# New issue orders for the attention steps of a decoder block, and an earlier load of the second pair's context

## The chip, the core and the metric

The kernel runs on one core of a Trainium2 chip, with all 32 sequences of the batch on that core. The metric is the device time of a run in microseconds (us); lower is better. Times are medians of several runs, and beside them stands one profiled execution with a trace of every instruction.

## The reference

A decoder block in float32 over x of shape (32, 128, 256): causal linear self-attention, cross-attention to a context of the same shape, and a feed-forward part with four gated or GELU layers, each behind a layer norm and with a residual sum. Cut to what matters:

```python
q, k = elu(xn @ Wq.T + bq) + 1, elu(xn @ Wk.T + bk) + 1     # 16 heads of 16
v = xn @ Wv.T + bv
out = sum_{t<=s} (q_s . k_t) v_t / (sum_{t<=s} q_s . k_t + 1e-6)
x = x + out @ Wo.T + bo
attn = softmax(q2 @ k2.T * 0.25)      # q2 from layernorm(x), k2 and v2 from the context
x = x + attn @ v2
h = silu(w1(xn) * s1) * (w2(xn) * s2); h = gelu(h1(h)); h = gelu(h2(h)); x = x + w3(h)
```

## The kernel before

**Tiling.** The batch is worked in 16 pairs of sequences (2 x 128 tokens). Self-attention (functions a_...) of pair m and cross-attention (b_...) of pair m-3 run in the same step m; there are 20 steps (SKEW is 3). The feed-forward part follows in 8 blocks of four sequences; its first block begins beside the last attention steps. Self-attention is computed as masked scores: scores (tile sa) times a causal 0/1 matrix (tile at, line 536) and then times the values (tile pf, line 413), with a column of ones that gives the denominator. Cross-attention computes its scores twice: once for the row maxima (tile sm, then DVE at line 603), and once with the maxima subtracted (tile se, whose last four matmuls add the maxima mT, then the exponential on ACT into tile pr, line 639).

**An order written by hand.** Every function is a generator. It issues one engine's part and yields: a_queries issues its matmuls on PE at the first call, its activations on ACT at the second, the sum on DVE at the third, the masking by heads on POOL at the fourth. A list such as both names units in the order in which they are called, as (function, pairs ahead, half), and give walks through it. So the list sets the order of work on PE, ACT, DVE and POOL, each of which takes its instructions strictly in that order. norms has six calls: three statistics on DVE (with the deviations at the third), the power on POOL, and the normed tiles xna and xnb on POOL. Lists: head ahead of the first step; first0, first1 and first2 for steps 0 to 2, where there is no cross-attention to do yet; both for the full steps 3 to 14; close for step 15; begins, alone, last and rest for steps 16 to 19, in which beside issues a block of feed-forward matmuls and settle its activations.

**Buffers that order the work.** The three kinds of scores of either half share one pair of PSUM tiles (ps_s, two banks each). All other matmul results rotate through four banks (ps_m). The masked scores at have one buffer for each tile of the pair:

```python
at = buffer([P, 2, 4, S], F32, tag=f"at{u}", name="at", bufs=1)
```

One buffer each also have the transposed inputs xTa and xTb, e, r, pr and kb2. The context cT has two. b_load fetches a pair's context (256 KB) from the SP queue:

```python
def b_load(m):
    cT = buffer([P, DC, 2 * S], F32, tag="cT", name="cT")
    nc.sync.dma_start(out=cT, in_=ctxT[:, ts(m, 2 * S)].rearrange("(c p) t -> p c t", p=P))
```

**Names used below.** Projections: tile pp (line 368: a_keys, a_queries, b_keys, b_queries) and pv (line 376: a_values, b_values); pt (line 357) are transposes of normed tiles, pz (line 613) the transpose of the maxima, pot (line 652) that of b_out, pw (line 376) the output projection of a_out. fa and fb (line 430) are transposed results, oa and ob their quotients on POOL, oT and oTb transposed back on DVE (line 445). vb are the context's values in SBUF, kb and kb2 its keys; qa and ka are queries and keys of self-attention. Line 831 is a row of 20 transposes that keeps PE busy till the first data are there.

Of the kernel before, what the change touches and what calls it, by code (L numbers as in the profile page):

```python
# [9 lines left out]
F32 = mybir.dt.float32  # L10
# [6 lines left out]
P = 128  # L17
# [27 lines left out]
def decoder_block_kernel(  # L45
# [222 lines left out]
    with tc.manual_schedule(engines=ORDERED):  # L268
# [24 lines left out]
        cT0 = buffer([P, DC, 2 * S], F32, tag="cT", name="cT")  # L293
# [10 lines left out]
        nc.sync.dma_start(out=row, in_=rows.partition_broadcast(P))  # L304
        load_w(nc.sync, 3)
# [376 lines left out]
        def settle():  # L682
# [9 lines left out]
            (b_keys, 0), (a_norm, 0), (b_keys, 0), (a_norm, 0), (b_values, 0), (a_transpose, 0),  # L692
            (a_norm, 1), (a_transpose, 0), (a_norm, 1), (a_queries, 0), (a_queries, 0), (b_values, 0),
            (a_queries, 0), (a_values, 0), (a_keys, 0), (a_transpose, 1), (a_values, 0), (a_queries, 0),
            (a_keys, 0), (a_transpose, 1), (a_keys, 0),
        ]
        first0 = [
            (norms, 0), (norms, 0), (a_scores, 0, 0), (a_bias, 0), (a_scores, 0, 0), (norms, 0),
            (a_keys, 1), (a_scores, 0, 1), (a_scores, 0, 1), (norms, 0), (norms, 0), (a_weighted, 0, 0),
            (a_keys, 1), (norms, 0), (a_keys, 1), (a_queries, 1), (a_weighted, 0, 0),  # L700
            (a_weighted, 0, 1), (a_values, 1), (a_queries, 1), (a_weighted, 0, 1), (a_queries, 1),
            (a_weighted, 0, 0), (a_transpose, 2), (a_weighted, 0, 1), (a_transpose, 2),
            (a_weighted, 0, 0), (a_values, 1), (a_queries, 1), (a_out, 0, 0), (a_weighted, 0, 1),
            (a_out, 0, 0), (a_bias, 2),
        ]
        first1 = [
            (a_bias, 0), (norms, 0), (a_scores, 0, 0), (a_out, -1, 1), (a_scores, 0, 0), (a_keys, 1),
            (a_out, -1, 1), (norms, 0), (a_keys, 1), (norms, 0), (norms, 0), (a_scores, 0, 1),
            (a_scores, 0, 1), (a_weighted, 0, 0), (a_keys, 1), (a_queries, 1), (norms, 0),
            (a_weighted, 0, 0), (a_weighted, 0, 1), (a_values, 1), (a_weighted, 0, 0), (a_queries, 1),  # L710
            (a_weighted, 0, 1), (a_weighted, 0, 1), (norms, 0), (a_transpose, 2), (a_weighted, 0, 0),
            (a_weighted, 0, 1), (a_values, 1), (a_queries, 1), (a_out, 0, 0), (a_queries, 1),
            (a_transpose, 2), (a_bias, 2), (a_out, 0, 0),
        ]
        first2 = [
            (a_out, -1, 1), (a_out, -1, 1), (a_keys, 1), (a_keys, 1), (a_scores, 0, 0), (norms, 0),
            (b_transpose, 1), (b_transpose, 1), (a_scores, 0, 0), (norms, 0), (norms, 0), (norms, 0),
            (a_values, 1), (a_weighted, 0, 0), (a_scores, 0, 1), (a_weighted, 0, 0), (a_weighted, 0, 0),
            (b_queries, 1), (a_scores, 0, 1), (b_load, 2), (a_values, 1), (a_keys, 1), (norms, 0),
            (b_queries, 1), (a_queries, 1), (a_weighted, 0, 1), (norms, 0), (a_weighted, 0, 0),  # L720
            (a_queries, 1), (a_out, 0, 0), (a_weighted, 0, 1), (a_queries, 1), (a_weighted, 0, 1),
            (b_queries, 1), (a_out, 0, 0), (a_queries, 1), (a_weighted, 0, 1),
# [3 lines left out]
            (a_transpose, 1), (b_maxima, 0, 0), (b_transpose, 1), (b_values, 1), (b_maxima, 0, 0),  # L726
# [59 lines left out]
            (b_out, 0, 0), (norms, 0),  # L786
        ]
        rest = [
            (b_weighted, -1, 1), (b_weighted, -1, 1), (norms, 0), (b_weighted, -1, 1), (norms, 0),
            (b_weighted, -1, 1), settle, beside, (b_out, -1, 1), (b_out, -1, 1), (b_out, -1, 1), settle,  # L790
            (norms, 0),
        ]
# [268 lines left out]
```

## Time and profile before

| what | value |
|---|---|
| median of three runs | 1090.45 us (1090.17 to 1090.6) |
| profiled execution | 1090.98 us |
| its span, first to last instruction | 1088.9 us |
| busy in the span | PE 99%, DVE 55%, POOL 37%, ACT 35% |
| full step (both), start to start | 25.92 us |
| first b maxima (step 3 begins) | at 60.32 us |
| close begins | at 370.98 us |
| begins, alone, last begin | at 392.51, 414.15, 434.97 us |
| granted PE clock | 0.998 over the span |

The attention steps take up to about 456 us, the feed-forward part the rest. In the timeline a row is: start in us, duration in us, engine, line, operation, result<-operands, shapes, count, and in brackets the idle time before it and what ended it. Ends of matmuls are modelled, so the distance between two starts on PE tells more than a duration. In the stretches the columns are: stretch, length, busy time of PE, PE's weight loads, DVE, ACT and POOL with the number of instructions, the granted clock, the DMA share and GB/s. Matmuls on strips (32 of 128 rows for scores, 32 columns for pf) run up to four at a time.

### The profile page before, as it was taken

The numbers are of one execution on the slowest core, as the hardware profiler recorded it, in microseconds if no ns is written. First come the engines' busy times: TensorE is split into PE (matmuls) and PEld (weight loads), VectorE is DVE, ScalarE is ACT, GpSimd is POOL, SyncE is SP. The second block draws the span as 40 slices with busy tenths as digits, with TensorE's granted clock in tenths as the row PEclk, the third lists the DMA queues.
The fourth block names the chain that finished last, engine by engine and source line by source line (L and its number), as shares of the span: only waits on it lengthen the run. The fifth ranks groups of instructions, "written<-read, shape, count | busy, mean of one in ns | idle before, by whom it ended". The sixth has DMA issues, their size and how long they took to land.

```text
span 1088.9 us, 19303 instructions
## 1 busy us (share of the span) xinstructions
PE 1077.3 (99%) x7990; PEld 876.9 (81%) x7990; DVE 599.0 (55%) x1210; ACT 377.8 (35%) x594; POOL 404.8 (37%) x648
## 2 busy tenths in 40 slices
PE   8999999999999999999999999999999999999998
PEld 6777777777777777788888888888888888888887
DVE  4888888888888877523433433433433432423422
ACT  3234444444444459832322322312312312312311
POOL 5555455554544436652312312312312312312311
PEclk9999999999999999999999999999999999999999
DMA  8000001001110000051011011011011000000000
GB/s 266 2 30 31 30 31 31 30 30 39 42 31 30 11 11 2 20 193 35 25 39 34 25 39 35 25 39 39 21 39 39 20 30 20 11 10 20 11 1 23
DMA packets 26542, 39.21 MB, mean 36 GB/s; under 512 B 2512, under 2 KB 18640, under 8 KB 26448
## 3 DMA queue, kind: packets, MB, share of 16 engines
q1 hardware_dynamic: 22000, 26.09, 7.1%
q0 software_dynamic: 4032, 11.54, 3.3%
q8 instruction: 65, 1.06, 0.4%
q10 hardware_dynamic: 416, 0.28, 0.1%
q14 instruction: 29, 0.24, 0.1%
HBM read 33.71 MB, written 4.19 MB: 35 GB/s over the span
## 4 chain that ended last, share of the span: by engine, by line
PE 97%; DVE 2%; POOL 1%; issue 0%; ACT 0%; DVEq 0%; POOLq 0%
PE ph L224 53%; PE pp L368 10%; PE py L885 6%; PE pf L413 5%; PE pv L376 5%; PE sa L397 4%; PE sm L397 3%; PE se L397 3%; PE pw L376 2%; PE pt L357 1%; PE pot L652 1%; PE se L628 1%; PE pz L613 1%; PE pt L213 1%; DVE at L536 1%; PE idle L831 0%
## 5 line engine op out<-in xcount | busy, mean ns | idle before, releaser
L189 DVE TENSOR_TENSOR gl<-hg,gh 128x512 fp32r<-128x512 f32 x126 | 87.3, 693 | 335.0 <-POOL gh L188 332.1
L248 ACT ACTIVATE hg<-ph,col 128x512 f32<-128x512 f32 x128 | 88.3, 690 | 361.3 <-PE ph L224 361.2
L188 POOL CAST gh<-hg 128x512 fp32r<-128x512 f32 x128 | 79.8, 623 | 359.0 <-ACT hg L248 358.9
L224 PE MATMUL ph<-sh,H 128*128 128x512 f32 x512 | 199.6, 390 | 0.0
L224 PE MATMUL ph<-sl,H 128*128 128x512 f32 x512 | 199.3, 389 | 0.0
L224 PE MATMUL ph<-gh,H 128*128 128x512 f32 x512 | 199.2, 389 | 0.0
L224 PE MATMUL ph<-gl,H 128*128 128x512 f32 x512 | 199.2, 389 | 0.0
L224 PEld LDWEIGHTS ph<-sh,H 128*128 128x128 f32 x512 | 96.1, 188 | 20.4 <-issue 0.5
L224 PEld LDWEIGHTS ph<-gl,H 128*128 128x128 f32 x512 | 96.1, 188 | 20.0
L224 PEld LDWEIGHTS ph<-sl,H 128*128 128x128 f32 x512 | 96.1, 188 | 20.0
L224 PEld LDWEIGHTS ph<-gh,H 128*128 128x128 f32 x512 | 96.1, 188 | 19.9
L224 PE MATMUL ph<-xh,W 128*128 128x512 f32 x256 | 100.7, 393 | 0.0
L224 PE MATMUL ph<-xl,W 128*128 128x512 f32 x256 | 99.8, 390 | 0.0
L603 DVE TENSOR_REDUCE nm<-sm 128x8 f32<-128x1024 f32 x64 | 75.2, 1217 | 17.9 <-PE sm L397 17.9
L188 POOL CAST sh<-hs 128x512 fp32r<-128x512 f32 x64 | 58.5, 914 | 69.2 <-DVE hs L240 69.2
L536 DVE TENSOR_TENSOR at<-sa,causal 128x1024 f32<-128x1024 f32 x64 | 74.5, 1206 | 15.6 <-PE sa L397 11.9
L639 ACT ACTIVATE pr<-se 128x1024 f32<-128x1024 f32 x64 | 62.0, 1020 | 29.6 <-PE se L628 29.6
L240 DVE SCALAR_TENSOR_TENSOR hs<-ph,col,sil 128x512 f32<-128x512 f32 x64 | 47.9, 749 | 41.6 <-ACT sil L238 21.0
L495 ACT ACTIVATE e<-pp,col 128x256 f32<-128x256 f32 x64 | 26.9, 470 | 124.7 <-PE pp L368 94.2
L238 ACT ACTIVATE sil<-ph,col 128x512 f32<-128x512 f32 x64 | 44.1, 690 | 74.9 <-PE ph L224 74.8
L368 PE MATMUL pp<-xTa,WA 128*128 128x256 f32 x256 | 62.5, 388 | 0.7 <-ACT xTa L360 0.7
L885 PE MATMUL py<-W,gh 128*128 128x256 f32 x256 | 62.6, 285 | 0.0
(132 smaller groups left out, 1812.8 us busy)
## 6 DMA issues: line engine op xcount, KB each, us to landing
x<-in_x_dram SPq DMA_DIRECT2D x16, 256.0 KB, 5.7
cT<-in_ctxT_dram SPq DMA_DIRECT2D x16, 256.0 KB, 2.6
H<-in_h1T_dram POOLq DMA_DIRECT2D x8, 512.0 KB, 3.6
H<-in_h2T_dram POOLq DMA_DIRECT2D x8, 512.0 KB, 6.7
out_dram<-y SPq DMA_DIRECT2D x32, 128.0 KB, 1.7
raw<-in_h1T_dram SPq DMA_DIRECT2D x16, 256.0 KB, 2.6
raw<-in_h2T_dram SPq DMA_DIRECT2D x16, 256.0 KB, 2.6
WA<-in_wattn_dram SPq DMA_DIRECT2D x4, 256.0 KB, 4.7
```

The lines of the kernel that those rows point to most:

```text
L188: (high_engine.copy if high_engine is nc.scalar else high_engine.tensor_copy)(high, t)
L189: lows.append(lambda: low_engine.tensor_tensor(low, t, high.bitcast(F32), ALU.subtract))
L224: nc.tensor.matmul(pp, lhsT=w[:, k, ts(c, P)], rhs=parts[p], start=(k == 0 and p == 0), stop=(k == len(src) - 1 and p == 1),)
L248: nc.scalar.activation(t, pp, AF.Gelu, scale=col[:, c_scale + c : c_scale + c + 1])
L368: nc.tensor.matmul(pp[:, c, :], lhsT=w[:, d, ts(c, P)], rhs=src[:, d, :], start=(d == 0), stop=(d == DC - 1))
L376: nc.tensor.matmul(pp, lhsT=src[:, d, :], rhs=w[:, d, :], start=(d == 0), stop=(d == DC - 1))
L397: nc.tensor.matmul(sc[g // 2][:, g % 2, 2 * c : 2 * c + 2, :], lhsT=loaded[32 * g : 32 * g + 32, c, ts(j, S)], rhs=streamed[32 * g : 32 * ...
L413: nc.tensor.matmul(pf[32 * g : 32 * g + 32, i, :], lhsT=v[:, 8 * (i // 2) + 2 * g + i % 2, :], rhs=weights[g // 2][:, g % 2, i, :], start= ...
L536: nc.vector.tensor_tensor(at.rearrange("p g i s -> p (g i) s"), sc[u].rearrange("p g i s -> p (g i) s"), causal.unsqueeze(1).to_broadcast( ...
L603: nc.vector.tensor_reduce(nm[:, 2 * u : 2 * u + 2, :], sc[u], AX.X, ALU.max, negate=True)
L639: nc.scalar.activation(pr, sc[u], AF.Exp)
L885: nc.tensor.matmul(py[:, :D], lhsT=h[k][p][:, ts(j, S)], rhs=W3[:, k, :], start=(k == 0 and p == 0), stop=(k == HC - 1 and p == 1),)
```

## The change

The lists head, first0 to first2, both, close, begins, alone, last and rest get other orders of the same units. In both the second half's scores (a_scores, 0, 1) now come ahead of the first half's (a_weighted, 0, 0), with (a_queries, 1) between the first b_weighted and these scores; a_out of the step before comes ahead of the first a_scores; b_load stands at the end of the step. The context of the second pair is loaded in the first row of transfers (cT1), and its b_values is issued in head; so b_load fetches three pairs ahead (3 for 2) in first2 and both, and is gone from close. The work is the same otherwise. The diff, without first1, first2, begins, alone and rest:

```diff
@@ -290,7 +290,7 @@
                 out=WA[:, n] if n < 4 else WB[:, n - 4], in_=wattn[n].rearrange("(c p) o -> p c o", p=P)
             )
 
-        cT0 = buffer([P, DC, 2 * S], F32, tag="cT", name="cT")
+        cT0, cT1 = (buffer([P, DC, 2 * S], F32, tag="cT", name="cT") for _ in range(2))
         load_w(nc.scalar, 5)
         load_x(1)
         nc.sync.dma_start(out=cT0, in_=ctxT[:, : 2 * S].rearrange("(c p) t -> p c t", p=P))
@@ -302,6 +302,7 @@
         load_w(nc.sync, 1)
         load_w(nc.sync, 2)
         nc.sync.dma_start(out=row, in_=rows.partition_broadcast(P))
+        nc.sync.dma_start(out=cT1, in_=ctxT[:, 2 * S : 4 * S].rearrange("(c p) t -> p c t", p=P))
         load_w(nc.sync, 3)
         load_x(2)
         load_w(nc.sync, 4)
@@ -689,105 +690,105 @@
 
         prologue = SKEW
         head = [
-            (b_keys, 0), (a_norm, 0), (b_keys, 0), (a_norm, 0), (b_values, 0), (a_transpose, 0),
-            (a_norm, 1), (a_transpose, 0), (a_norm, 1), (a_queries, 0), (a_queries, 0), (b_values, 0),
-            (a_queries, 0), (a_values, 0), (a_keys, 0), (a_transpose, 1), (a_values, 0), (a_queries, 0),
-            (a_keys, 0), (a_transpose, 1), (a_keys, 0),
+            (b_keys, 0), (a_norm, 0), (b_values, 0), (a_norm, 0), (b_values, 0), (a_transpose, 0),
+            (a_transpose, 0), (a_norm, 1), (a_queries, 0), (b_keys, 0), (a_keys, 0), (a_queries, 0),
+            (a_queries, 0), (a_values, 0), (a_norm, 1), (a_queries, 0), (a_values, 0), (a_keys, 0),
+            (b_values, 1), (b_values, 1), (a_transpose, 1), (a_transpose, 1), (a_keys, 0),
         ]
         first0 = [
-            (norms, 0), (norms, 0), (a_scores, 0, 0), (a_bias, 0), (a_scores, 0, 0), (norms, 0),
-            (a_keys, 1), (a_scores, 0, 1), (a_scores, 0, 1), (norms, 0), (norms, 0), (a_weighted, 0, 0),
-            (a_keys, 1), (norms, 0), (a_keys, 1), (a_queries, 1), (a_weighted, 0, 0),
-            (a_weighted, 0, 1), (a_values, 1), (a_queries, 1), (a_weighted, 0, 1), (a_queries, 1),
-            (a_weighted, 0, 0), (a_transpose, 2), (a_weighted, 0, 1), (a_transpose, 2),
-            (a_weighted, 0, 0), (a_values, 1), (a_queries, 1), (a_out, 0, 0), (a_weighted, 0, 1),
-            (a_out, 0, 0), (a_bias, 2),
+            (norms, 0), (norms, 0), (norms, 0), (a_scores, 0, 0), (a_keys, 1), (norms, 0),
+            (a_scores, 0, 0), (norms, 0), (norms, 0), (a_scores, 0, 1), (a_keys, 1), (a_keys, 1),
+            (a_scores, 0, 1), (a_queries, 1), (a_queries, 1), (a_weighted, 0, 0), (a_weighted, 0, 1),
+            (a_weighted, 0, 0), (a_bias, 2), (a_queries, 1), (a_weighted, 0, 1), (a_bias, 0),
+            (a_transpose, 2), (a_values, 1), (a_weighted, 0, 0), (a_weighted, 0, 0), (a_values, 1),
+            (a_weighted, 0, 1), (a_weighted, 0, 1), (a_out, 0, 0), (a_out, 0, 0), (a_queries, 1),
+            (a_transpose, 2),
         ]
...
         both = [
-            (a_transpose, 1), (b_maxima, 0, 0), (b_transpose, 1), (b_values, 1), (b_maxima, 0, 0),
-            (b_out, -1, 1), (a_scores, 0, 0), (a_transpose, 1), (b_transpose, 1), (b_turn_maxima, 0, 0),
-            (a_scores, 0, 0), (b_out, -1, 1), (a_keys, 1), (b_values, 1), (b_turn_maxima, 0, 0),
-            (w_load, 0), (norms, 0), (a_out, -1, 1), (b_scores, 0, 0), (a_keys, 1), (b_queries, 1),
-            (a_out, -1, 1), (b_scores, 0, 0), (b_queries, 1), (b_maxima, 0, 1), (norms, 0),
-            (b_weighted, 0, 0), (b_out, -1, 1), (b_queries, 1), (norms, 0), (b_maxima, 0, 1),
-            (a_keys, 1), (b_load, 2), (a_weighted, 0, 0), (a_scores, 0, 1), (b_turn_maxima, 0, 1),
-            (a_bias, 1), (norms, 0), (norms, 0), (b_weighted, 0, 0), (a_scores, 0, 1),
-            (b_turn_maxima, 0, 1), (a_weighted, 0, 0), (b_weighted, 0, 0), (a_queries, 1),
-            (a_queries, 1), (b_weighted, 0, 0), (b_keys, 1), (b_scores, 0, 1), (a_values, 1),
-            (a_weighted, 0, 0), (a_weighted, 0, 1), (a_queries, 1), (norms, 0), (b_scores, 0, 1),
-            (a_weighted, 0, 0), (a_values, 1), (a_weighted, 0, 1), (b_weighted, 0, 1),
-            (b_weighted, 0, 1), (b_keys, 1), (b_out, 0, 0), (b_out, 0, 0), (a_weighted, 0, 1),
-            (a_weighted, 0, 1), (b_weighted, 0, 1), (a_out, 0, 0), (b_out, 0, 0), (a_out, 0, 0),
-            (a_queries, 1), (b_weighted, 0, 1),
+            (b_maxima, 0, 0), (b_maxima, 0, 0), (a_transpose, 1), (b_values, 1), (a_transpose, 1),
+            (b_transpose, 1), (w_load, 0), (b_transpose, 1), (a_out, -1, 1), (a_scores, 0, 0),
+            (b_values, 1), (a_out, -1, 1), (b_out, -1, 1), (b_turn_maxima, 0, 0), (a_scores, 0, 0),
+            (a_keys, 1), (b_turn_maxima, 0, 0), (b_scores, 0, 0), (b_out, -1, 1), (a_keys, 1),
+            (b_scores, 0, 0), (b_out, -1, 1), (norms, 0), (b_queries, 1), (norms, 0), (norms, 0),
+            (a_keys, 1), (b_maxima, 0, 1), (norms, 0), (b_weighted, 0, 0), (a_queries, 1),
+            (b_maxima, 0, 1), (a_scores, 0, 1), (a_weighted, 0, 0), (b_queries, 1), (b_weighted, 0, 0),
+            (norms, 0), (a_scores, 0, 1), (b_turn_maxima, 0, 1), (b_keys, 1), (b_turn_maxima, 0, 1),
+            (a_queries, 1), (a_queries, 1), (b_scores, 0, 1), (b_scores, 0, 1), (a_weighted, 0, 0),
+            (a_values, 1), (b_weighted, 0, 0), (b_queries, 1), (b_weighted, 0, 0), (a_bias, 1),
+            (a_values, 1), (a_weighted, 0, 0), (norms, 0), (a_weighted, 0, 1), (b_keys, 1),
+            (b_weighted, 0, 1), (b_out, 0, 0), (a_queries, 1), (b_out, 0, 0), (a_weighted, 0, 0),
+            (a_weighted, 0, 1), (a_weighted, 0, 1), (a_out, 0, 0), (b_weighted, 0, 1),
+            (b_weighted, 0, 1), (a_weighted, 0, 1), (a_out, 0, 0), (b_weighted, 0, 1), (b_out, 0, 0),
+            (b_load, 3),
         ]
         close = [
-            (b_maxima, 0, 0), (b_out, -1, 1), (b_transpose, 1), (a_out, -1, 1), (w_load, 0),
-            (b_maxima, 0, 0), (a_scores, 0, 0), (b_transpose, 1), (b_out, -1, 1), (a_out, -1, 1),
-            (b_values, 1), (a_scores, 0, 0), (b_turn_maxima, 0, 0), (b_turn_maxima, 0, 0),
-            (b_values, 1), (b_scores, 0, 0), (b_scores, 0, 0), (norms, 0), (a_weighted, 0, 0),
-            (b_keys, 1), (b_out, -1, 1), (norms, 0), (b_maxima, 0, 1), (a_weighted, 0, 0),
-            (b_queries, 1), (norms, 0), (b_maxima, 0, 1), (b_load, 2), (norms, 0), (a_scores, 0, 1),
-            (a_scores, 0, 1), (b_turn_maxima, 0, 1), (a_weighted, 0, 0), (b_weighted, 0, 0),
-            (b_turn_maxima, 0, 1), (b_weighted, 0, 0), (b_weighted, 0, 0), (a_weighted, 0, 0),
-            (b_scores, 0, 1), (b_queries, 1), (b_keys, 1), (a_weighted, 0, 1), (b_weighted, 0, 0),
-            (a_weighted, 0, 1), (a_out, 0, 0), (norms, 0), (b_queries, 1), (a_out, 0, 0), (b_out, 0, 0),
-            (b_scores, 0, 1), (b_out, 0, 0), (a_weighted, 0, 1), (b_out, 0, 0), (norms, 0),
+            (b_transpose, 1), (b_maxima, 0, 0), (a_out, -1, 1), (b_out, -1, 1), (b_maxima, 0, 0),
+            (a_scores, 0, 0), (a_out, -1, 1), (b_turn_maxima, 0, 0), (b_out, -1, 1), (b_transpose, 1),
+            (a_scores, 0, 0), (b_values, 1), (b_turn_maxima, 0, 0), (b_scores, 0, 0), (b_scores, 0, 0),
+            (w_load, 0), (norms, 0), (a_weighted, 0, 0), (norms, 0), (b_out, -1, 1), (norms, 0),
+            (b_maxima, 0, 1), (a_weighted, 0, 0), (a_weighted, 0, 0), (b_maxima, 0, 1),
+            (b_weighted, 0, 0), (norms, 0), (b_values, 1), (b_queries, 1), (a_scores, 0, 1),
+            (b_turn_maxima, 0, 1), (b_weighted, 0, 0), (a_scores, 0, 1), (b_turn_maxima, 0, 1),
+            (b_queries, 1), (a_weighted, 0, 0), (b_keys, 1), (b_weighted, 0, 0), (norms, 0),
+            (b_keys, 1), (b_weighted, 0, 0), (b_queries, 1), (b_scores, 0, 1), (a_weighted, 0, 1),
+            (b_out, 0, 0), (b_scores, 0, 1), (a_weighted, 0, 1), (a_out, 0, 0), (a_weighted, 0, 1),
+            (norms, 0), (b_out, 0, 0), (a_out, 0, 0), (b_out, 0, 0),
         ]
...
         last = [
-            (b_maxima, 0, 0), (b_maxima, 0, 0), (norms, 0), settle, beside, (b_weighted, -1, 1),
-            (b_weighted, -1, 1), (b_weighted, -1, 1), (b_turn_maxima, 0, 0), (b_turn_maxima, 0, 0),
-            (b_scores, 0, 0), settle, (b_scores, 0, 0), (b_weighted, -1, 1), (norms, 0), beside,
-            (b_weighted, 0, 0), (b_out, -1, 1), settle, (b_maxima, 0, 1), (b_weighted, 0, 0), beside,
-            (b_maxima, 0, 1), (b_turn_maxima, 0, 1), (b_weighted, 0, 0), (b_out, -1, 1),
-            (b_weighted, 0, 0), (b_turn_maxima, 0, 1), (b_out, -1, 1), settle, (b_scores, 0, 1),
-            (norms, 0), (norms, 0), (norms, 0), (b_out, 0, 0), beside, (b_scores, 0, 1), (b_out, 0, 0),
-            (b_out, 0, 0), (norms, 0),
+            (b_maxima, 0, 0), (b_maxima, 0, 0), (b_weighted, -1, 1), (b_turn_maxima, 0, 0),
+            (b_weighted, -1, 1), settle, beside, (norms, 0), (b_weighted, -1, 1), (b_turn_maxima, 0, 0),
+            (norms, 0), (b_weighted, -1, 1), settle, (b_scores, 0, 0), beside, (b_scores, 0, 0),
+            (b_out, -1, 1), (b_weighted, 0, 0), settle, (b_weighted, 0, 0), (b_out, -1, 1),
+            (b_maxima, 0, 1), (b_maxima, 0, 1), beside, (b_out, -1, 1), (b_turn_maxima, 0, 1),
+            (b_weighted, 0, 0), (b_turn_maxima, 0, 1), (b_scores, 0, 1), (b_weighted, 0, 0),
+            (b_out, 0, 0), settle, (b_scores, 0, 1), (b_out, 0, 0), (norms, 0), (norms, 0), beside,
+            (norms, 0), (norms, 0), (b_out, 0, 0),
         ]
...
@@ -820,8 +821,8 @@
             for c in range(FILLS - 1 - HC)
         ]
 
-        Bs[0]["c"] = cT0
-        done = {(b_load, 0)}
+        Bs[0]["c"], Bs[1]["c"] = cT0, cT1
+        done = {(b_load, 0), (b_load, 1)}
         constants()
         for v in (vb[0], va[0], va[1], vb[1]):
             fill(v)
```

## The prediction

> **What bounds the kernel now.** I read the page's chain first: its share by engine is nearly all TensorE.
>
> ```profile
> PE 97%; DVE 2%; POOL 1%; issue 0%; ACT 0%; DVEq 0%; POOLq 0%
> ```
>
> A chain of 97% PE does not say that PE is short of nothing: a matmul that waits between its first and last part counts as busy. The stretches show that the full steps repeat every 25.92 us, with DVE busy 22.68 us in each.
>
> ```profile
> 203.84:229.76 25.92, 25.92 (x306) 20.18 (x302) 22.68 (x49) 11.65 (x21) 13.29 (x23) 1.00 0.10 32
> 229.76:255.68 25.92, 25.92 (x306) 20.19 (x302) 22.68 (x49) 11.64 (x21) 13.28 (x23) 1.00 0.10 32
> ```
>
> So I went to the timeline of one full step, PE's rows and then DVE's, and measured from start to start. The three kinds of scores (sm, sa, se) share one pair of PSUM tiles, so each must be emptied before the next is filled.
>
> ```profile
> 203.84 1.61 PE L397 MATMUL sa<-qa,ka 32*128 32x256 f32 x16
> 205.38 0.33 PE L613 MATMUL pz<-ident,z 128*128 128x128 f32 x1
> ...
> 209.10 1.15 PE L397 MATMUL se<-qb,kb 32*128 32x256 f32 x16
> ...
> 215.88 1.15 PE L397 MATMUL sm<-kb,qb 32*128 32x256 f32 x16
> ...
> 219.49 1.15 PE L397 MATMUL sa<-qa,ka 32*128 32x256 f32 x16
> ...
> 220.67 2.36 DVE L536 TENSOR_TENSOR at<-sa,causal 128x1024 f32<-128x1024 f32 x2 [0.83 <-PE sa L397]
> ...
> 223.42 1.15 PE L397 MATMUL se<-qb,kb 32*128 32x256 f32 x16
> ...
> 226.65 1.29 PE L397 MATMUL sm<-kb,qb 32*128 32x256 f32 x16
> ```
>
> The reader is to see two things. Masking takes 1.18 + 2.36 = 3.54 us from the start of a self-attention score, so se cannot be filled entirely before +3.59 (DVE's end to the next weight load is about 0.05). And only one score of the step is visibly held: the sa at 203.84 needs 1.54 us to the next operation, the sa at 219.49 only 1.07 (next start 220.56). The 0.47 is the wait for the maxima (L603, done at 204.27). Everything else is PE's own cadence. (Columns: start, duration, engine, line.)
>
> Next, two places at the start of the trace:
>
> ```profile
> 18.82 1.15 PE L397 MATMUL sa<-qa,ka 32*128 32x256 f32 x16 [2.04 <-DVE ka L500]
> 19.90 3.58 PE L368 MATMUL pp<-xTa,WA 128*128 128x256 f32 x8
> ...
> 20.00:23.40 3.40, 3.40 (x8) 2.19 (x8) 2.57 (x5) 0.00 (x0) 0.71 (x1) 0.52 0.71 248
> ...
> 38.13 1.08 PE L413 MATMUL pf<-at,va 128*32 128x128 f32 x32
> ...
> 39.25 2.36 DVE L536 TENSOR_TENSOR at<-sa,causal 128x1024 f32<-128x1024 f32 x2 [0.76 <-PE pf L413]
> ...
> 41.66 1.07 PE L413 MATMUL pf<-at,va 128*32 128x128 f32 x28 [0.18 <-DVE at L536]
> ```
>
> First: PE idles 2.04 us before the first scores, and then a projection takes 3.50 us to the next start instead of 1.82, at a granted clock of 0.52. Second, the row on which this forecast rests: the at tiles have one buffer each, and where the second masking of a pair is put before the first pf has read them, the masking waits for that pf to end. From the pf's start to the next PE work that needs the result: 41.66 - 38.13 = 3.53 us.
>
> **The full steps (m = 4 to 14, eleven of them).** No operation is added or removed, so I lay the new PE order out with the cadences of the present step: projection 1.73 (1.82 ahead of a score or behind one; 1.92 ahead of sm or pf), score 1.07 ahead of whole-array work or of pf, sm behind pr 1.23 (its own 0.16 wait included), mT part .53 after the .78 of its scores, pf .90 ahead of pf, 1.01 ahead of a projection (24.53 to 25.54), .99 ahead of pot, pw .96 ahead of a score and .87 otherwise, pot .27, pz .17, pt .44 to .53. From score to score:
>
> - sm0 to sa0: before 3.61. New: sm 1.08, pt .49, b values 1.73, pt .44, pw .96 = 4.70. The maxima are ready at about 3.6 to 3.9, so no wait.
> - sa0 to se0: before 3.93. New: 1.07, pot .27, pz .17, keys 1.82 = 3.33; the pw that stood here has gone ahead of sa0. Below the 3.59 of masking: wait .26, so 3.59.
> - se0 to sm1: 3.23 both times.
> - sm1 to sa1: before 3.11, and then .47 inside sa1. New: 1.23, pf of b 1.01, the a queries 1.92 = 4.16. DVE has the three statistics (3.65) and now ka ahead of the maxima; these end about 3.8 after sm1's start, so the .47 is gone.
> - sa1 to se1: before 5.26 (with that .47). New: 1.07, then the pf of a, 1.01, pz .17, b keys 1.82 = 4.07. But this pf is the one that reads the at tiles, so masking starts only at its end: 1.07 + 1.08 + .03, two times 1.18, .05 = 4.59, as in the rows at 38 to 41 us. Wait .52. mT follows on DVE at 5.2, in time for its matmul at 5.37.
> - se1 to the next sm0: before 6.78. New: .78, .53, a values 1.92, .90, .99, .27, pw .96 = 6.35.
>
> Before 25.92, new 26.62: +0.70 a step, of which +.31 is waits (.26 + .52 - .47) and +.39 cadence (the array goes between row strips, column strips and whole use 16 times instead of 14). Eleven steps: +7.7.
>
> What could add to it: each queue is reordered too. DVE idles some 1.3 us at the new wait; behind it stand mT, the queries' e, fa and the rest. Walked through, fa of the first half ends 0.8 us before pf needs its bank, oT 0.9 before pw, and oTb is late by 0.3 into the next step's maxima, where sa0 has slack of about 0.8. DVE's 22.7 of work plus 1.3 is below 26.6. POOL (13.3 busy) makes qa 4 us ahead of its use. ACT's kb tiles free pot's bank as now (212.85 + 1.29 against pot at 214.21), the order from se1 to pot being the same. So I add nothing for these; the cover is the slack named, and beyond it (0.8 us for oTb and oT) the step loses the excess.
>
> **Loads.** The context load moves from the middle of a step to its end, but fetches one pair further ahead: it has nearly a step where a load lands in 2.6 us. Its wait (for the keys that last read the buffer) holds up only SP, and SP has nothing else to do till the output. At the start one more issue (about 0.5 us of SP) and 256 KB (0.7 us at 383 GB/s) come ahead of WO, the third pair and XQ. x of the third pair then lands near 12 us and is read at 18, WO is read at 32. Cost 0; lower bound 0, upper bound 0.7 if something were that close.
>
> **Head and first steps.** In the head the second pair's values (1.73) go ahead of the first scores. ACT puts vb ahead of xTa (+0.1), and kb, kb2 between xTa and the exponentials: the keys' bank is free at 12.85 instead of 12.7. PE then runs on: queries 11.0, keys 12.9, values 14.6, b values 16.3, transposes 18.1, first scores about 18.6, where ka (17.8) and qa (16.7) are ready. So the 2.04 idle is filled. By the Trainium skill, "TensorE: Matmul & The Clock Gate", section "HAM oscillation — how this bites in real kernels", only PE gaps above about 3.4 us matter to the clock; then filling 2.04 us is worth those 2.04 at most. The row above disagrees: after 2.04 us of idleness the clock was about half for 3.4 us, and the projection took 1.68 longer. I take the row, so 1.7 more.
>
> The new first step gives it back. Its queries stand ahead of the first pf, so (same at tiles) the second masking starts at 26.2 instead of 25.64 and the second pf goes on at 28.6 instead of 28.05; PE has only four matmuls between 26.0 and 28.6. From there to the second pair's keys: 35.2 against 35.24 now. The second and third step come out the same way: the first b maxima at 60.5 against 60.32, with one transpose (.5) owed and the values done. The first full step lacks those values but its sa0 must wait for the maxima (3.58 after sm0), so it gains only 1.1 of the 1.73 against the new steady step: 25.5. Sum to its end, the owed transpose counted: +0.1. Bounds: -3.4 if both fillings came through (1.73 + 1.68), +1.7 if the gap at 26 to 28.6 halves the clock once more (by the skill's rule it would not, by the row it can).
>
> **The last steps.** close now has its scores 1.3 behind the first maxima, 0.4, 1.2 and 0.5 later on; walked likewise it takes 22.2 us against 21.6: +0.6. begins and alone hang on ACT's table loads (three and a half us each around a silu), whose number is unchanged: -0.2. In last, pz now stands ahead of settle and of a block of eight matmuls, and waits about 1.8 us for the maxima on DVE, half of it made up: +0.9. Bounds of the three: -1.5 and +3. The feed-forward part (from 460 us) is untouched.
>
> **Sum.** +0.1 + 7.7 + 0.6 + 0.7 = +9.1 us. The profiled execution took 1090.98 (span 1088.9 and 2.1 around it), so 1100.1; the median of the runs is 0.5 lower, so 1099.5.
>
> **Rivals.** (1) Other side: the score tiles' halves are released one by one and four matmuls start ahead, so the .26 and .52 are hidden; the old .47 is gone all the same and cadence costs less than counted. A step then takes 25.8 or less, eleven give -1 to -3, and the head gives -1.5: about 1087.5. For it: DVE has 3 us of slack a step. Against it: in the rows at 38 to 41 us just this wait held PE despite those four matmuls. It decides where a step falls under 25.8. Chance 0.11. (2) A second bound: DVE's late oTb and oT push maxima and pw, each step loses 0.3 to 0.6 more (eleven times: 3 to 7 us), the clock's 1.7 on top at worst: 1103 to 1107. For it: nearly every DVE slack above is under 1 us. Chance 0.12. (3) The new order is a wash, the waits about .2 in all, steps at 25.9 to 26.1: 1090 to 1092.5. Chance 0.09. That the change doesn't do what it says is no rival here: orders are issued as written.
>
> **Numbers.** The forecast itself, +0.4 to +0.95 a step, has 0.68 and covers 1095 to 1102.5. 0.2% is 2.2 us, about what a measurement of this kernel can tell from no change: faster 0.10, same 0.08, slower 0.82. The range 1091.5 to 1104.5 leaves out most of rival 1 and the upper part of rival 2.
>
> **What would show it.** In the changed trace: the period of full steps at 26.6; at (L536) waiting for pf (L413) about 1.2 us once a step; se held by DVE at twice a step, and the sa behind the second maxima no longer split; no clock dip at 20 us; a wait of PE near 26 to 28.6 us. A period at 25.9 or less, or an at that does not wait for pf, would make the prediction wrong.

## The result and the profile after

The changed kernel takes 1097.51 us (median of 4 runs, 1096.6 to 1098.02), the kernel before in the same session 1090.53 (4 runs, 1090.17 to 1090.81): a ratio of 1.0064, interval 1.0052 to 1.0076. It is 7.0 us slower. The forecast was 1099.5. The profiled execution took 1097.93 us with a span of 1095.8, so 6.9 us more span than before (1088.9).

All lines of the code stand one lower than before: scores L398, pf L414, at L537, maxima L604.

In the chain of the changed kernel, TensorE's share is still nearly everything, so by that view nothing has happened:

```profile
PE 96%; DVE 1%; issue 0%; ACT 0%; POOL 0%; DMA 0%; SPq 0%; POOLq 0%; DVEq 0%
```

The stretches do tell it. Here are two full steps, from one sm to the same sm of the next step (length; busy time and count of PE, PEld, DVE, ACT, POOL; granted clock; DMA share; GB/s):

```profile
192.99:219.45 26.46, 26.46 (x303) 20.02 (x302) 22.48 (x49) 11.53 (x21) 13.32 (x23) 1.00 0.11 32
219.45:245.92 26.47, 26.47 (x303) 20.04 (x303) 22.48 (x49) 11.53 (x21) 13.33 (x23) 1.00 0.10 31
```

A step has nearly the same work (weight loads 20.0 us against 20.2 before, DVE 22.5 against 22.7) and takes 26.465 us instead of 25.92 (the mean of ten steps, 87.13 to 351.79). PE counts as busy in all of it, although it waits: the waits lie within groups of matmuls. The timeline of PE in the first of these steps shows them as cuts (start, duration, engine, line, operation):

```profile
192.99 1.15 PE L398 MATMUL sm<-kb,qb 32*128 32x256 f32 x16
...
197.68 1.15 PE L398 MATMUL sa<-qa,ka 32*128 32x256 f32 x16
...
200.96 1.23 PE L398 MATMUL se<-qb,kb 32*128 32x256 f32 x14
...
202.57 1.99 PE L369 MATMUL pp<-xTb,WB 128*128 128x256 f32 x8
...
204.49 1.16 PE L398 MATMUL sm<-kb,qb 32*128 32x256 f32 x16
...
208.51 1.15 PE L398 MATMUL sa<-qa,ka 32*128 32x256 f32 x16
209.59 1.08 PE L414 MATMUL pf<-at,va 128*32 128x128 f32 x32
210.60 0.33 PE L614 MATMUL pz<-ident,z 128*128 128x128 f32 x1
...
212.59 1.44 PE L398 MATMUL se<-qb,kb 32*128 32x256 f32 x14
214.41 1.99 PE L377 MATMUL pv<-WA,xTa 128*128 128x256 f32 x8
```

Both se are broken after 14 of their matmuls (x14 where an undisturbed one shows x16). The first needs 1.61 us to the next operation, the second 1.82, where an undisturbed one needs 1.31 (16 matmuls on strips in 0.78 us, four at a time, where 8 on the whole array take 1.73; then the four for the maxima): waits of 0.30 and 0.51. The sa behind the second maxima, which was cut before, is whole. The first cut is the one that was forecast: masking ends 3.54 us after its score starts, and se comes after 3.28. DVE's timeline has the reason for the second; the bracket is the idle time before the operation and what ended it:

```profile
210.71 2.35 DVE L537 TENSOR_TENSOR at<-sa,causal 128x1024 f32<-128x1024 f32 x2 [1.13 <-PE pf L414]
```

The masking starts 1.12 us after pf does, at its end, not at the end of the scores. DVE keeps to the listed order meanwhile: the inputs of the queries' sum e were ready at 210.19 (the end of L498 on ACT), with DVE idle, and e ran at 213.58, behind the masking. The list of costliest groups names the new releaser too (busy in all, ns of one; then the idle time ahead and what ended most of it). First the kernel before, where it was the scores, then the changed one:

```profile
L536 DVE TENSOR_TENSOR at<-sa,causal 128x1024 f32<-128x1024 f32 x64 | 74.5, 1206 | 15.6 <-PE sa L397 11.9
L537 DVE TENSOR_TENSOR at<-sa,causal 128x1024 f32<-128x1024 f32 x64 | 75.3, 1218 | 26.1 <-PE pf L414 17.0
```

The trace of the tile se names DVE's masking as what PE's weight loads for se waited for 13 times (3.0 us in all); in experiment 1 below, only once (0.2 us).

At the start, PE's timeline of the changed kernel and three stretches (same columns as above):

```profile
18.03 1.15 PE L398 MATMUL sa<-qa,ka 32*128 32x256 f32 x16
19.11 1.99 PE L369 MATMUL pp<-xTa,WA 128*128 128x256 f32 x8
...
24.61 1.08 PE L414 MATMUL pf<-at,va 128*32 128x128 f32 x32
...
27.00 0.41 PE L414 MATMUL pf<-at,va 128*32 128x128 f32 x4 [1.31 <-DVE at L537]
28.13 1.57 PE L414 MATMUL pf<-at,va 128*32 128x128 f32 x28 [0.72 <-DVE at L537]
```

```profile
20.00:23.40 3.40, 3.40 (x25) 2.28 (x24) 2.23 (x3) 1.57 (x4) 3.16 (x7) 1.00 0.83 287
26.00:30.00 4.00, 2.28 (x34) 1.61 (x35) 3.93 (x7) 0.28 (x1) 0.72 (x1) 0.82 0.00 0
30.00:34.00 4.00, 4.00 (x16) 3.15 (x14) 2.02 (x6) 0.59 (x1) 3.18 (x6) 0.76 0.00 0
```

The 2.04 us of idleness before the first scores are gone, and so is the half clock at 20 us. In their place PE idles 1.31 + 0.72 = 2.03 us in the first step, again for the masking, and the clock falls there. The first sm stands at 61.95 (before 60.32).

From there the starts of sm give the account, after against before:

| start of | after | before | difference |
|---|---|---|---|
| the first sm of step m = 4 | 87.13 | 86.27 | +0.86 |
| the same sm ten steps on | 351.79 | 345.49 | +6.30, so +5.44 in ten steps |
| begins' sm (behind the last full step and close) | 399.85 | 392.51 | +7.34 |
| alone's sm | 421.37 | 414.15 | +7.22 |
| last's sm | 441.16 | 434.97 | +6.19 |
| the sm after it | 451.91 | 445.00 | +6.91 |

The new list has its sm one transpose (0.5) earlier in the slot than the old one, so the first part really owes +1.36, and the eleventh step (+0.55) and close (about 0) make up the rest of the third row. Most of the loss is in the full steps. These are single executions: PE's second projection starts at 7.43 us here and at 7.89 before, where PE's order is still the same.

### The profile page after: what moved, and what is told of

Read it like the earlier page. It is cut to its first block, busy times and chain, and to the rows that moved or that the text cites. A ratio compares the mean times of both kernels' runs of the same rounds, so it can differ in the third digit from the quotient of the medians.

```text
span 1095.8 us, 19355 instructions
## 1 busy us (share of the span) xinstructions
PE 1082.6 (99%) x7990; PEld 875.2 (80%) x7990; DVE 596.4 (54%) x1210; ACT 375.7 (34%) x594; POOL 405.7 (37%) x648
## 4 chain that ended last, share of the span: by engine, by line
PE 96%; DVE 1%; issue 0%; ACT 0%; POOL 0%; DMA 0%; SPq 0%; POOLq 0%; DVEq 0%
PE ph L224 53%; PE pp L369 10%; PE py L886 6%; PE pf L414 5%; PE pv L377 5%; PE se L398 4%; PE sa L398 3%; PE sm L398 3%; PE pw L377 2%; PE pt L358 1%; PE se L629 1%; PE pot L653 1%; PE pt L213 1%; DVE nm L604 1%; PE pz L614 1%
## 5 line engine op out<-in xcount | busy, mean ns | idle before, releaser
L537 DVE TENSOR_TENSOR at<-sa,causal 128x1024 f32<-128x1024 f32 x64 | 75.3, 1218 | 26.1 <-PE pf L414 17.0
L604 DVE TENSOR_REDUCE nm<-sm 128x8 f32<-128x1024 f32 x64 | 74.7, 1207 | 7.9 <-PE sm L398 7.9
L886 PE MATMUL py<-W,gl 128*128 128x256 f32 x256 | 62.0, 283 | 0.0
```

The costliest lines, as they stand in the source:

```text
L537: nc.vector.tensor_tensor(at.rearrange("p g i s -> p (g i) s"), sc[u].rearrange("p g i s -> p (g i) s"), causal.unsqueeze(1).to_broadcast( ...
L604: nc.vector.tensor_reduce(nm[:, 2 * u : 2 * u + 2, :], sc[u], AX.X, ALU.max, negate=True)
L886: nc.tensor.matmul(py[:, :D], lhsT=h[k][p][:, ts(j, S)], rhs=W3[:, k, :], start=(k == 0 and p == 0), stop=(k == HC - 1 and p == 1),)
```

## The experiments

**1. Two buffers for the first at tile.** The disputed wait is removed by what makes it: with a second buffer the masking need not wait until pf has read the first. The first at tile alone gets one, and qa gives up its second buffer to make room. The order of the work is that of the changed kernel.

```
- two = buffer([P, DC, 2, 2 * S], F32, tag=tag, name=tag)
+ two = buffer([P, DC, 2, 2 * S], F32, tag=tag, name=tag, bufs=1 if tag == "qa2" else 2)
...
- at = buffer([P, 2, 4, S], F32, tag=f"at{u}", name="at", bufs=1)
+ at = buffer([P, 2, 4, S], F32, tag=f"at{u}", name="at", bufs=2 - u)
```

> The changed kernel with two buffers for the first of the two at tiles (and one in place of two for qa, to make room). The second masking can then begin while pf still reads the first half's scores. My theory (masking waits for pf, and se waits for masking): the wait of at for pf, 1.13 us a step, and the 0.52 us by which the second se of a step is held are gone; a full step takes 25.95 us in place of 26.47; eleven steps give 5.7 us, and the first step's gap shrinks: 1097.5 falls to about 1091.5. Rival (the loss is the extra switching between row strips, column strips and the whole array, and the waits are covered): period 26.3 to 26.5, time 1096 to 1098. Rival of the second bound (DVE): the wait comes back elsewhere, period 26.2 or more.

Measured: 1089.08 us (21 runs), ratio to before 0.9993 (0.9986 to 0.9999). By the ratios that is 0.7% or 7.7 us below the changed kernel: the whole loss. PE's timeline of one step, and DVE's masking in it:

```profile
229.60 1.15 PE L398 MATMUL sa<-qa,ka 32*128 32x256 f32 x16
230.67 1.08 PE L414 MATMUL pf<-at,va 128*32 128x128 f32 x32
...
233.67 1.15 PE L398 MATMUL se<-qb,kb 32*128 32x256 f32 x16
234.98 1.99 PE L377 MATMUL pv<-WA,xTa 128*128 128x256 f32 x8
```

```profile
230.78 2.36 DVE L537 TENSOR_TENSOR at<-sa,causal 128x1024 f32<-128x1024 f32 x2
```

The masking starts 1.18 us after sa instead of 2.20, with no idle bracket, se is whole, and 1.31 us on comes the next operation. The period is 25.955 (214.07 to 240.02): 0.51 less, just the wait that was seen. The other cut, se behind the first masking, was still there (222.05 to 223.64, 1.59 us), since it does not come from the buffer:

```profile
222.05 1.23 PE L398 MATMUL se<-qb,kb 32*128 32x256 f32 x14
...
223.64 1.99 PE L369 MATMUL pp<-xTb,WB 128*128 128x256 f32 x8
```

Twelve steps (m = 3 to 14) give 6.1. Another 2.3 in the two profiles (8.4 together) are ahead of them (first sm at 59.63 instead of 61.95), where the same wait stood: more than had been expected. The time fell 2.4 us below the expected 1091.5.

**2. The same buffers in the kernel before (control).** If at's second buffer were good in itself, experiment 1 would prove little.

> The kernel before the change with two buffers for the first at tile and one for qa, the same edit as in the first experiment. My theory: in the old order pf reads the first half's scores ahead of the second half's sa, so in the full steps nothing waits for the at buffers: period 25.92 as before; only the first steps, where pf stood behind that sa, gain: 1089.3 to 1090.5. Rival (a second buffer is worth as much in any order): period 25.4 or less, 1085.

Measured: 1089.01 (13 runs), ratio 0.9984 (0.9976 to 0.9992). The period stayed at 25.92. The gain of about 1.7 us is all ahead of the full steps (first sm at 58.52 instead of 60.32). In the profiles 0.28 of it stands already at the first sa (18.54 instead of 18.82). So in the old order the full steps do not wait for this buffer; the new order made the wait.

**3. The wait of the first se.** Here the projection pw goes back between sa0 and se0, where it stood before.

```
- (a_out, -1, 1), (a_scores, 0, 0), (b_values, 1), (a_out, -1, 1), (b_out, -1, 1),
+ (a_scores, 0, 0), (b_values, 1), (b_out, -1, 1),
...
+ (a_keys, 1), (a_out, -1, 1), (b_turn_maxima, 0, 0), (b_scores, 0, 0), (a_out, -1, 1), (b_out, -1, 1),
```

> The changed kernel with the output projection of the step before (a_out, -1, 1) put back between the keys and the first se of the full steps, where it stood before the change. My theory: se then comes 0.9 us later after sa, masking (3.54 us) is done, the 0.30 us by which the first se is held is gone, and the score ahead of it still comes no sooner than the maxima are ready (3.83 against 3.75 us): period 26.17, eleven steps give 3.3 us: 1094.2. Rival (cadence alone): 26.4 to 26.5, 1097. If the maxima are late: sa is held instead, period 26.3 to 26.5.

Measured: 1097.13 (5 runs), ratio 1.0059 (1.0045 to 1.0072): the expected total was missed. PE's timeline of a step:

```profile
226.60 1.15 PE L398 MATMUL se<-qb,kb 32*128 32x256 f32 x16
...
227.91 1.99 PE L369 MATMUL pp<-xTb,WB 128*128 128x256 f32 x8
229.84 1.30 PE L398 MATMUL sm<-kb,qb 32*128 32x256 f32 x16
231.06 1.08 PE L414 MATMUL pf<-pr,vb 128*32 128x128 f32 x32
```

The first se is whole, 1.31 us to the next operation: the 0.30 is gone. But now sm takes 1.22 us to the next start instead of 1.09. The exponentials pr, which empty the score tiles, end at 229.95 here, 0.11 after sm starts; in the changed kernel they end 0.03 ahead of it (204.46 and 204.49), because the held se had delayed sm. Half of the gain goes to this next wait: the period is 26.30 instead of 26.465, where 26.17 was expected. In its profile the eleven steps give 1.8 us (begins' sm at 398.03 instead of 399.85, with the sm of step 4 where it was), and `last` takes 1.6 of it back: from its sm to the next 12.32 us instead of 10.75, at a clock of 0.93 and 0.73 in the two stretches of 5 us there. The list `last` is the same in both kernels (see below).

**4. pf taken away from between the scores.** In place of another buffer, another order: the pf that reads at goes ahead of the queries and sa1. Its transposition on DVE, further down in the list, moves ahead too.

```
- (a_queries, 1), (b_maxima, 0, 1), (a_scores, 0, 1), (a_weighted, 0, 0), (b_queries, 1),
+ (a_weighted, 0, 0), (a_queries, 1), (b_maxima, 0, 1), (a_scores, 0, 1), (b_queries, 1),
```

> The changed kernel with the first pf of self-attention ahead of the queries and of the second half's sa in the full steps (and its transposition on DVE ahead of the queries' e, so that its bank is free in time). Masking no longer waits for pf, but only pz and one projection are left between sa and se, 3.06 us against the 3.59 that masking takes. My theory: the second se is held by 0.53 all the same, a step takes 26.3 to 26.4 us, time 1096. Rival (the wait for pf alone held se): period 25.85, 1090.5.

Measured: 1096.76 (4 runs), ratio 1.0049 (1.0034 to 1.0065), with a period of 26.33, as expected. PE's timeline, then DVE's:

```profile
207.95 1.15 PE L398 MATMUL sa<-qa,ka 32*128 32x256 f32 x16
209.03 0.33 PE L614 MATMUL pz<-ident,z 128*128 128x128 f32 x1
...
211.02 1.44 PE L398 MATMUL se<-qb,kb 32*128 32x256 f32 x14
212.84 1.99 PE L377 MATMUL pv<-WA,xTa 128*128 128x256 f32 x8
```

```profile
209.13 2.35 DVE L537 TENSOR_TENSOR at<-sa,causal 128x1024 f32<-128x1024 f32 x2 [1.03 <-PE sa L398]
```

The masking starts 1.18 us after sa, as in experiment 1, and yet se is cut and takes 1.82 us. With pf gone, PE arrives at se after 3.07 us, and the masking needs 3.59 before the score tiles are free. It is the same 0.5, now for the score tiles. pf was both what delayed the masking and what PE did meanwhile. Of the two remedies tried, the buffer takes the one and leaves the other; no run put other work between sa and se.

**5. The old full steps in the changed kernel.** What do the other parts cost alone? `both` is that of before, with the load at its end.

> The changed kernel with the full steps' order of before (only the load of the context stays at the end of the step, three pairs ahead). My theory: the loss is in the eleven full steps: period 25.92, time 1091.0 to 1091.7; what is left is the head and the first steps. Rival (the loss is in the head, the first and the last steps): 1095 or more.

Measured: 1094.47 (5 runs), ratio 1.0035 (1.0021 to 1.0048): a miss, 3 us above what was expected and nearer to the rival's 1095. The period is 25.92. But begins' sm stood at 394.67, 2.2 us behind the kernel before, all from the first steps (first sm at 62.46); and the first full step took 25.89, although the values of the second pair were done: PE reached sa0 earlier and waited for the maxima. Another 1.6 us came in `last`, where the clock fell to 0.66 and sm to sm took 12.35 us instead of 10.75.

**6. The first steps: gap and clock apart.** Experiments 6a and 6b part the two. 6a lays 18 transposes with unused results into the gap, which leaves the wait of the masking but keeps PE busy. 6b removes the wait: the first pf goes ahead of the two blocks of queries. The rule that 6a's expectation sets against its theory is the one that the prediction quotes.

```
6a: - (a_queries, 1), (a_weighted, 0, 0), (a_weighted, 0, 1),
    + (a_queries, 1), (a_weighted, 0, 0), keep_busy, (a_weighted, 0, 1),
6b: - (a_scores, 0, 1), (a_queries, 1), (a_queries, 1), (a_weighted, 0, 0), (a_weighted, 0, 1),
    + (a_scores, 0, 1), (a_weighted, 0, 0), (a_queries, 1), (a_queries, 1), (a_weighted, 0, 1),
```

> The changed kernel with 18 transposes of the identity between the first pf of the first step and the second, where PE stands idle for 2.3 us (they are extra work, read by nobody, 1.9 us at full clock). My theory (the idle time halves the granted clock from 28 to 32 us[...]): the clock stays at 1.00, the first maxima of cross-attention come at 60.4 us in place of 61.95, and the time falls by 1.2 to 1.7 us: 1096. By the rule[...]: no change, or slower by up to 0.5 us.

> The changed kernel with one unit moved in the first step: the first pf ahead of the second pair's queries instead of behind them. My theory (the second masking waits for that pf, so the queries in between delay everything after): masking of the second half starts at 23.8 instead of 26, the second pf goes on at 26.2 instead of 28.1, PE has no idle gap there, the clock stays at 1.00 from 26.8 to 33.6 us, the first maxima come at 59.5 to 60.3 us, and the time falls by 1.2 to 1.8 us: 1095.7 to 1096.3. Rival (another wait, for qa or oT, takes its place in the second step): 1097 or more.

Measured: 6a 1097.09 (5 runs), ratio 1.0061 (1.0047 to 1.0074); 6b 1095.45 (5 runs), 1.0043 (1.0029 to 1.0057). 6a's total missed the expected 1096; 6b's came out a little below what was expected. The first pf rows of 6b:

```profile
22.60 1.08 PE L414 MATMUL pf<-at,va 128*32 128x128 f32 x32
...
26.12 1.07 PE L414 MATMUL pf<-at,va 128*32 128x128 f32 x28 [0.18 <-DVE at L537]
```

The second pf goes on at 26.12 instead of 28.13. In 6a's profile the first sa stands 0.9 us later than in the changed kernel's, ahead of anything that the edit touches. The stretch from the first sa to the first sm is free of that, and with it the runs with this first step fall into three sets:

| | first sa | first sm | between |
|---|---|---|---|
| gap, clock reduced: changed kernel | 18.03 | 61.95 | 43.92 |
| the same: experiment 8 | 17.94 | 61.87 | 43.93 |
| gap, clock 1.00: experiment 3 | 18.94 | 61.27 | 42.33 |
| the same: experiment 4 | 18.85 | 61.17 | 42.32 |
| gap filled with transposes, clock 1.00: 6a | 18.97 | 61.30 | 42.33 |
| wait removed: 6b | 17.95 | 58.31 | 40.36 |
| wait removed by the buffer: experiment 1 | 18.99 | 59.63 | 40.64 |

(Experiment 5 is left out: in its list one more transpose stands ahead of the first sm.) The wait costs 1.7 to 2.0 us, and the reduced clock 1.6 more where it comes. 6b cuts both from the changed kernel's profile (3.56). The median fell by only 2.1: in 6b's profile, too, the clock fell in `last`, to 0.69 (sm to sm 12.29).

**7. The new head alone, in the kernel before**, with the load that it needs:

> The kernel before the change with only its new head and the early load of the second context: the second pair's values are projected ahead of the first scores, all later orders as before. What the head gains: no 2.04 us of idle PE ahead of the first scores and no halved clock from 20 to 23.4 us; first maxima of cross-attention at 58.6 us in place of 60.3. My theory: the values were hidden in the wait for the maxima of the first full step, so that step stays at 25.9 us and their 1.73 us are not gained a second time: 1088.7 to 1089.3. Rival (the head is worth both, 3.4 us): 1087. Rival (it is worth nothing, the first steps give it back even in the old order): 1090.3 or more.

Measured: 1090.13 (13 runs), ratio 0.9998 (0.999 to 1.0006): no difference that can be measured, where 1088.7 to 1089.3 was expected. PE's timeline at the first full step:

```profile
58.74 1.15 PE L398 MATMUL sm<-kb,qb 32*128 32x256 f32 x16
59.81 0.66 PE L358 MATMUL pt<-ident,xnb 128*128 128x128 f32 x4
62.33 1.18 PE L398 MATMUL sa<-qa,ka 32*128 32x256 f32 x16 [1.86 <-DVE nm L604]
```

The clock at 20 to 23.4 us is 1.00 instead of 0.52, and the first sm comes 1.58 us earlier. The values (1.73) that were projected early bring nothing on top: the first full step still takes 25.95, because sa0 waits 1.86 us for the maxima just where they stood. The profiled execution (1089.19) keeps the 1.58 to its end; in the median it isn't seen. The clocks on record tell part of why: the seven runs with a clock of 0.999 or 1.000 over the span took 1089.2 to 1090.1, the six with 0.998 took 1090.6 to 1091.0. The kernel before does the same without the new head: in all comparisons together, its seven runs with 1.000 took 1089.4 to 1089.7, its forty with 0.998 took 1090.2 to 1091.9. So much of what the new head gives in its profile may be a dip of the clock that the kernel before does not have in every execution. Where the clock fell in the six is open, as only one run has a trace.

**8. The old `last` in the changed kernel.**

> The changed kernel with the order of before in the last step but one (the list last). My theory: PE's wait for z ahead of pz, 1.9 us, goes, half of which was made up later: -0.9, and the clock cannot drop there any more: 1096.0 to 1096.7. Rival (the last steps play no part): 1097.3 or more.

Measured: 1097.62 (5 runs), ratio 1.0058 (1.0045 to 1.0072): no gain, a miss. In `last`, sm to sm takes 10.55 us with the old list, 10.75 with the new, 10.03 in the kernel before. ACT's timeline of this experiment:

```profile
441.43 1.28 ACT L238 ACT_TABLE_LOAD   x1
...
443.43 1.28 ACT L81 ACT_TABLE_LOAD   x1
...
448.35 1.92 ACT L640 ACTIVATE pr<-se 128x1024 f32<-128x1024 f32 x2
```

PE's rows of it (the transpose of the maxima, then the pf that reads pr):

```profile
445.81 0.33 PE L614 MATMUL pz<-ident,z 128*128 128x128 f32 x1 [0.42 <-DVE hs L240]
...
450.32 1.07 PE L414 MATMUL pf<-pr,vb 128*32 128x128 f32 x28 [0.16 <-ACT pr L640]
```

The long wait ahead of pz (1.90 us in the changed kernel) is gone with the old list, and yet only 0.2 us come back. ACT has no gap from 439.20 to 453.69; two silu with two table loads each (1.28 us a load) stand in line ahead of pr, and PE waits for pr. So 0.5 of the 0.7 that `last` loses is not in its list. PE comes out of `alone` 1.0 us sooner, and ACT does not: in the kernel before it starts the first of these loads at 433.88, 1.09 us ahead of sm, and then idles 0.73 for se ahead of pr; here it starts it at 441.43, 0.29 behind sm. What would make ACT's part shorter was not tested.

**9. Better versions.** 9a joins the buffers of experiment 1, pw of experiment 3 and the old `last`. 9b is the kernel before with the same buffers and only the full steps of 9a (its context load after the keys), so against experiment 2 it changes the full steps alone.

> The changed kernel with two buffers for the first at tile (one for qa), the pw of the step before back ahead of the first se, and the old list last. My theory: period 25.78 (25.955 of the first experiment, less the 0.30 of the first se, plus 0.13 that sm then waits for the exponentials), eleven steps give 1.9 us, last another 0.9: 1086.3. Rival (DVE, at 22.7 us a step, or the score tiles set a floor of 25.9): 1088.2 or more.

> The kernel before the change (its head, first steps, closing steps and loads) with two buffers for the first at tile, one for qa, and only the full steps of the best version so far (the changed order with pw back ahead of the first se). My theory: the good of the change lies in its full steps once at has a second buffer, and its head, first and last steps are worth nothing in sum: period 25.79, time 1087.2 to 1087.8, as the best version. Rival (the changed head and ends are worth 1.5 us): 1088.8 or more.

Measured: 9a 1087.57 (6 runs, 1087.14 to 1088.01), ratio 0.997 (0.9957 to 0.9982); 9b 1087.71 (9 runs, 1086.4 to 1088.31), 0.9974 (0.9964 to 0.9984). Both beat both kernels, and neither the other. 9b is within what was expected. A step takes 25.79 us in both. One step of 9a on PE:

```profile
213.61 1.15 PE L398 MATMUL sm<-kb,qb 32*128 32x256 f32 x16
...
221.59 1.15 PE L398 MATMUL se<-qb,kb 32*128 32x256 f32 x16
...
224.82 1.29 PE L398 MATMUL sm<-kb,qb 32*128 32x256 f32 x16
...
233.05 1.15 PE L398 MATMUL se<-qb,kb 32*128 32x256 f32 x16
```

No se is cut any more. So the new order of the full steps, freed of its two waits, is 0.13 us a step better than the old one, and the new head, first and closing lists are worth nothing in sum that these runs could tell (9a against 9b). 9a missed its expectation by 1.3 us, most of it the 0.9 that experiment 8 had been supposed to give and did not.

## Why the prediction was right

Its main step holds: at waits for pf once a step (1.13 us; 1.2 was named), that cuts se by 0.51 (0.52), and the other se by 0.30 (0.26). Experiment 1 shows that it is this wait and decides sign and size: without it, the kernel is not slower. The old cut of 0.47 is gone, as said. That the total came so near (6.9 us in the profiles against 9.1) is in part luck: the first part came out 1.3 us dearer than forecast, the other terms 3.4 cheaper. By its own terms:

- **Full step, +0.70.** Measured +0.545. From score to score (predicted, then measured): 4.70, 4.69; 3.33, 3.28; 3.49, 3.53; 4.16, 4.02; 4.07, 4.08; 6.87, 6.86. One term was mis-sized, sm1 to sa1, which charged sm 0.16 for a wait for pr. With se held for 0.30 just before, pr is ready (0.03 us ahead of sm). Experiment 3 shows the two to be one exchange: free se and sm waits. Eleven steps: +6.0 in place of +7.7.
- **First part, +0.1.** Measured +1.36. The filling of the 2.04 gap worked, clock included, and the new gap in the first step came where it was put (26 to 28.6 predicted, 25.7 to 28.1 seen). The term that failed is its clock, valued at 0 with 1.7 as the upper bound. The upper bound came true: 43.92 - 42.33 = 1.6. With it, and with the 0.5 by which this execution was ahead before the orders differ, the forecast would have been 0.1 + 1.6 - 0.5 = 1.2. The Trainium skill ("TensorE: Matmul & The Clock Gate", "HAM oscillation — how this bites in real kernels") gives as its rule "no PE-idle gaps >~3.4µs"; by it the shorter gaps here would cost only their own length, but two idle stretches of 1.31 and 0.72 us were followed by a lower clock in three profiles, and in two others not (last section). The prediction had rejected that rule for the gap before the first scores, from the trace, and then spared the new gap what its own row showed. Nor does every execution seem to pay it: of the four runs of the changed kernel two (the profiled one is among them) had a clock of 0.997 over the span and took 1097.9 and 1098.0 us, two had 0.999 and took 1096.6 and 1097.1.
- **First full step.** It was put at 25.5, because sa0 must wait for the maxima; measured 25.18. Experiment 7 shows the mechanism in the old list: all 1.73 of the early values is lost there.
- **close, +0.6.** Measured about 0 once the transposed start of the slot is allowed for.
- **begins, alone, last: -0.2 and +0.9.** Measured -0.1, -1.0 and +0.7. The size for `last` is near, by luck: the wait for the maxima is there (1.90 us; 1.8 was named), but it is worth only 0.2. Experiment 8 has the old list, without this wait, and loses 0.5 to ACT's table loads all the same. The 1.0 that `alone` gains was not forecast, and most of it is what `last` then gives back to ACT.
- **Slack of DVE's queue.** Costed at nothing, and right: with 1.1 us of idleness each step in DVE, nothing behind it became the bound. The loads cost nothing that could be seen either.

Rival 1 (the waits are hidden by the four matmuls that start ahead) is refuted by the cut se rows and by experiment 1. Of rival 2, the clock part came true, the DVE part did not. Rival 3 is refuted by the period. The sum: 1.36 + 6.0 + 0 - 0.4 = 6.9 against 9.1.

## What to carry to other kernels

When an order is changed, look first at the tiles with one buffer: each consumer that is moved between two writes of such a tile ties the writer's queue to the consumer's end, and the price lands at the third party that needs the writer next (here se, held by DVE, held by pf: 0.51 us a step). Where the consumer is also the work that covers the writer's time, moving it out of the way can cost the same again (experiment 4), and a second buffer did not. And a wait taken out of a chain of waits brings only what is left when the next one shows (here 0.15 us of 0.30): follow the chain to that one before the gain is counted.

## What was not expected of the hardware

- A gap of 2 us on PE is followed by a lower clock in one execution and not in another of the same order: the changed kernel and experiments 5 and 8 have it in the first step (clock 0.76 to 0.82 in the stretches), experiments 3 and 4 with the same two idle times do not. Two stretches of experiment 3 (columns as above), to be read against those of the changed kernel:

```profile
26.00:30.00 4.00, 1.97 (x56) 1.27 (x45) 3.29 (x5) 1.20 (x4) 0.00 (x0) 1.00 0.00 0
30.00:34.00 4.00, 3.64 (x21) 2.87 (x19) 3.54 (x10) 0.59 (x1) 3.09 (x5) 1.00 0.01 2
```

- The two executions that kept the clock had come to this step 0.7 to 1.0 us later (first sa at 18.85 and 18.94, the others at 17.94 to 18.11). Whether that decides, no run tested.
- The same happens in `last`, where PE waits some 1.9 us: 12.3 us from sm to sm with a clock of 0.66 to 0.93 in experiments 3, 4, 5 and 6b, 10.75 with full clock in the changed kernel and in experiments 1 and 6a. That 1.6 us comes and goes with no edit near it, and in the profiles of experiments 3 and 5 it takes back part of what their steps gave.
- At the start of an execution, 20 idle transposes took 4.53 us in nine profiles and 3.77 to 4.11 in the other four, while the clock column says 1.00 in all thirteen.
